# A gated cross-attention block on one core: the first half's normalised tokens turned in 32-by-32 blocks by VectorE, a query copy placed between two exponentials, two more warming products

## The chip, the core and the metric

The kernel runs on one core of one Trainium2 chip. The core has five engines that run side by side and wait for each other only through semaphores: TensorE (PE, with its weight loads shown as PEld), VectorE (DVE), ScalarE (ACT), GpSimd (POOL) and SyncE (SP), which here does nothing but issue DMAs. The metric is the device time of one execution in microseconds (us), as the median of several executions. Before the change it is 1525.99 us (three runs, 1525.85 to 1526.12).

## What is computed

There are 32 sequences of 64 tokens with 512 features, so 2,048 tokens. The block is a gated cross-attention with 32 heads of 128, followed by a gated linear layer with low-rank adapters. Cut to what matters here:

```python
x = x + tanh(g_xattn[0]) * xattn(layernorm(x), ctx, mask, bias, Wq, Wk, Wv, Wo)
x = x + tanh(g_ffn[0]) * ffn(layernorm(x), weight, bias, lora_A, lora_B, starts)

# xattn: q = x @ Wq, k = ctx @ Wk, v = ctx @ Wv  (32 heads of 128)
#        probs = softmax(q k^T / sqrt(128) + position_bias, masked); ctx = probs v; return ctx @ Wo
# ffn:   y = x @ weight^T + bias, plus (x @ A^T) @ B^T for the sequences that have an adapter
```

The second layernorm reads the result of the attention, token by token. The linear layer needs those tokens with the features on the partitions, while the attention leaves them with tokens on the partitions, so they have to be turned.

## The kernel before

The tokens are worked in two halves, p = 0 and p = 1, of 1,024 tokens (eight tiles of 128 tokens, two chunks of 512). Each half goes through three stages:

- the key stage, 16 units n = 0 to 15, one for each pair of heads (`stage_a`, first loop);
- the value stage, 16 units (`stage_a`, second loop);
- the attention, 16 pairs of heads: a query unit, the scores, a softmax, the product with the values and the product with Wo, summed into eight tiles `acc` (`attention` and its `run`).

The linear layer follows at the end of half two for all four chunks c = 0 to 3 (`ffn_chunk`): chunks 0 and 1 are the first half's tokens, chunks 2 and 3 the second half's.

Products in full precision are made of three products of split operands: `split` makes a rounded high part on ACT (`nc.scalar.copy`) and the remainder on DVE or POOL, and `mm3` (L99) multiplies high by high, high by low and low by high. A `unit` (L356, L361, L378) is one matrix product by seven block products in the order p1, p6, p7, p5, p2, p4, p3, each of six matmuls of 512 columns. The last two of a unit are carried into the next one, so that the order on PE is p1 of unit n, then p4 and p3 of unit n-1, then p6, p7, p5, p2 of unit n. DVE or ACT takes each partial sum out of PSUM. Product p4 adds into the bank (`pv`) that DVE reads after p7, and p3 into the one (`pz`) that DVE reads after p5, so PE may not start them before those reads have ended.

The order of everything beside the products is written by hand. A side job is a generator; those under way stand in the list `streams`, and `beat()`, called after each block product, runs each of them up to its next `yield`. So a job's instructions are put in between the additions of the units, one step for each block product, and `drain(job)` issues what is left of it at once. Every engine, SP too, executes its instructions in the order of issue.

What the change touches:

- **The start.** PE multiplies the identity with itself eight times (L519, `warm`) before the first real products `ppk` (L407).
- **The end of half one.** The finished tiles `acc` go to the DRAM tensor `x1d`, 128 tokens of 2 KB each. In half two's key stage `acc_stats` takes their mean and variance (from n = 3, one tile every second beat), and in its value stage `acc_rstd` makes the reciprocal roots, a chain of small operations on 128x4 tiles, one to a beat (from g = 1, L735).
- **The linear layer.** `x1_load` brings `x1d` back with tokens on partitions. For each tile `ffn_norm` normalises it on DVE (L132) into `xn`, and `ffn_tile` turns it by four TensorE transposes into PSUM (L137, `tpf`), from which ACT takes the high part (L1237) and DVE the low one (L1238). Chunk 0's tiles are turned beside the last Wo products (`beside`), those of chunk c+1 inside `ffn_chunk(c)`.
- **The first softmax of each half.** Only here are scores (L838), exponentials (L848), row sums, the division, a block-wise transpose on DVE (L876) and the copies of the turned blocks (L873, ten on ACT and six as small DVE transposes) all waited for by the very next value product `po` (L985). Beside them runs query unit 1. In that unit ACT copies the first partial sum (L361) behind both exponentials.

Of the kernel before, what the change touches and what calls it, by code (L numbers as in the profile page):

```python
# [9 lines left out]
F32 = mybir.dt.float32  # L10
# [7 lines left out]
P = 128  # L18
# [25 lines left out]
def flamingo_block(ctx: ExitStack, tc: tile.TileContext, x, xT, ctxT, bias, mask, gx, gf,  # L44
# [30 lines left out]
    ident = const.tile([P, P], F32, name="ident")  # L75
    make_identity(nc, ident)
    x1d = dram.tile([NT * P, D], F32, name="x1d")
    kd = [[dram.tile([P, 2, TP], F32, name=f"kd{p}_{n}") for n in range(NPR)] for p in range(NPH)]
    lnd = [dram.tile([2, NT, P], F32, name=f"lnd{p}") for p in range(NPH)]
    vd = [[dram.tile([P, NT, 512], F32, name=f"vd{p}_{g}") for g in range(2 * NG)] for p in range(NPH)]  # L80
# [434 lines left out]
    for _ in load_ctx(0, f, KT):  # L515
        pass
    warm = psum("warm")
    for i in range(8):
        nc.tensor.matmul(warm[:, :P], ident, ident, start=True, stop=True)  # L519
    fetch("k", 1, "r1")  # L520
    first = {}, {}
# [157 lines left out]
    def acc_rstd(p):  # L679
        for c in range(p * NCH, (p + 1) * NCH):  # L680
            yield from ln_rstd(mv2[:, c * 4:(c + 1) * 4, :], f"f{c}", rstd, c, 5)
            yield

    def stage_a(p, first, fc, res, rot, more, enter, blocks):
        xc, plain = first
        f = None
        for n in range(NPR):
            g = p * NPR + n
            if n == 0 and plain:
                sums = sum_blocks(fc, res, f"c{p}", nc.vector, xc)  # L690
                streams.append(sums)
            if n == 0 and not plain:
                drain(blocks)
            if n == (1 if plain else 0):
                streams.append(key_blocks(p, n + 1))
            if n == 3:
                f = [big(f"f{j}", [P, KT, 512], F32, f"xf{p}_{j}") for j in range(2)]
                t7 = big(rot[7], [P, 2, 1024], F32, f"wvr{p}_0a")
                t8 = big(rot[8], [P, 2, 1024], F32, f"wvr{p}_0b")
                fetch_v(p, 0, [t7[:, 0], t7[:, 1], t8[:, 0], t8[:, 1]])  # L700
                if more:
                    streams.append(paced(more, 2))
                xstat = x_stats(p)
                streams.append(xstat)
            if n == 5:
                vsum = [None] + [rwp.tile([P, 1024], F32, tag=f"r{2 + i}", name=f"vs{p}_0_{i}") for i in range(2)] + [None]
                v0 = paced(blocks_v(p, 0, rot, vsum, nc.vector, K_ORDER), 3)
                streams.append(v0)
            if 6 <= n < 6 + KT:
                for j in range(NCH):  # L710
                    nc.sync.dma_start(out=f[j][:, n - 6, :], in_=xT[p * NCH + j, n - 6])
            if n == 10:
                drain(xstat)
                x_spread(p)
            kt = k_tile(g)
            w = wt[("k", g)]

            def store(kt=kt, n=n):
                for i in range(2):
                    nc.sync.dma_start(out=kd[p][n][:, i, :], in_=kt[:, i, :])  # L720
            if n < 2 and plain:
                for j in range(2):
                    plain_half(w, plain, k_dst(kt), f"k{g}", j, plain["ps"] if n == 0 and j == 0 else None)
                store()
            else:
                if n == 2 and plain:
                    drain(sums)
                carry[:] = [unit(w, xc, None, k_dst(kt), f"k{g}", tuple(carry)), store]
        drain(v0)
        xnorm = paced(x_norm(p, f), 2)  # L730
        streams.append(xnorm)
        xq = {}
        for g in range(NG):
            if g == 1 and p:
                streams.append(acc_rstd(p - 1))  # L735
            if g == 2:
                drain(xnorm)
                streams.append(mask_stream(p))
                if p == 0:
                    streams.append(adapt)  # L740
            if g == NG - 1:
                t4 = pieces(rwp.tile([P, 1024], F32, tag="r1", name=f"x{p}t4"))
                fetch("q", p * NPR, "r0")
                bias = enter()
                streams.append(turned_blocks(f, [rot[(7 * NG + i) % 9] for i in range(7)], f"x{p}", nc.gpsimd, keep,
                                             t4, xq, bias, enter))
            for t in range(4):
                if t == 1:
                    if g + 1 < NG:
                        raw = [rwp.tile([P, 1024], F32, tag=f"r{i}", name=f"wvr{p}_{g + 1}_{i}") for i in range(4)]  # L750
                        fetch_v(p, g + 1, raw)
                        streams.append(blocks_v(p, g + 1, rot, None, nc.gpsimd, V_ORDER))
                    if g == NG - 2:
                        keep = {}
                        streams.append(turned_sums(f, f"x{p}", nc.gpsimd, keep))
                if t == 2 and g == NG - 1:
                    streams.append(prep("q", p * NPR, nc.gpsimd))
                vt = kqp.tile([P, 4, 512], F32, tag="kq", name=f"vt{p}_{g}_{t}")
                dst = {(i, j): vt[:, i * 2 + j, :] for i in range(2) for j in range(2)}
                after = unit(wt["v", p, g], xc, slice(t * P, (t + 1) * P), dst, f"v{p}_{g}_{t}", tuple(carry))  # L760

                def store(vt=vt, g=g, t=t):
                    for i in range(2):
                        for j in range(2):
                            nc.sync.dma_start(out=vd[p][2 * g + i][:, j * 4 + t, :], in_=vt[:, i * 2 + j, :])
                carry[:] = [after, store]
        enter()
        return xq


    def attention(p, res, rest, qt, freed):
# [61 lines left out]
        def scores(n, i, qT, kT):  # L833
            ps = psum(f"ps{p}_{n}_{i}", (P, NT, S))
            for t in range(NT):
                for h in range(2):
                    tok = slice(t * P + h * S, t * P + (h + 1) * S)
                    nc.tensor.matmul(ps[h * S:(h + 1) * S, t, :], qT[:, i, tok], kT[:, i, tok], start=True, stop=True)  # L838
            s = sm[n % 2][:, i]
            nc.vector.scalar_tensor_tensor(s, ps, SCALE, s, ALU.mult, ALU.add)  # L840
            mx = st.tile([P, NT], F32, tag="mx", name=f"mx{p}_{n}_{i}", bufs=4)
            nc.vector.tensor_reduce(mx, s, AX.X, ALU.max)  # L842
            nc.gpsimd.tensor_tensor(s, s, mx.unsqueeze(2).to_broadcast([P, NT, S]), ALU.subtract)  # L843
            beat()
            if n:
                streams.append(exped(s))
            else:
                nc.scalar.activation(s, s, AF.Exp)  # L848
# [48 lines left out]
        def first_softmax():  # L897
            n = 0
            tp = [rows.tile([P, NT, S], F32, tag="row", name=f"tp{p}_{n}_{i}") for i in range(2)]
            norm = normed(n, 0, (1, 0))  # L900
            next(norm)
            yield
            next(norm)
            yield
            turn(tp[1], n, 1)
            turn(tp[0], n, 0)
            yield
            for q in quads:
                copy(nc.scalar.copy, n, 1, tp[1], *q)
            for q in quads[6:]:  # L910
                copy(nc.scalar.copy, n, 0, tp[0], *q)
            for q in quads[:6]:
                copy(nc.vector.transpose, n, 0, sm[0][:, 0], *q)
            yield
            load_bias(2)
            b["m", 2] = bias_mask(2, 16)
            streams.append(b["m", 2])
# [288 lines left out]
    def ffn_weights(tags):  # L1206
        wf = [big(tags[i], [P, KT, 512], F32R, f"wf{i}") for i in range(2)]
        ffn_w.update(wf=wf, tags=tags)
        ffn_w["xn"] = big(tags[6], [P, 4, D], F32, "xn")
        ar, br, a2 = ffn_w["ar"], ffn_w["br"], ffn_w["a2"]  # L1210

        b2 = ffn_w["b2"] = [wbp.tile([P, 512], F32R, tag="wb", name=f"b2{i}") for i in range(2)]
# [18 lines left out]
    def ffn_tile(c, t):  # L1231
        if t == 0:
            act[c] = [big(ffn_w["tags"][2 + 2 * (c % 2) + i], [P, KT, 512], F32R, f"fa{c}_{i}") for i in range(2)]
        hi, lo = act[c]
        ps = transposes(ffn_w["xn"][:, t, :], f"f{c}_{t}")
        h = hi[:, :, t * P:(t + 1) * P]
        nc.scalar.copy(h, ps)  # L1237
        nc.vector.tensor_tensor(lo[:, :, t * P:(t + 1) * P], ps, h.bitcast(F32), ALU.subtract)  # L1238

    def ffn_lora(c):  # L1240
        hi, lo = act[c]
# [34 lines left out]
    def ffn_chunk(c, beside=lambda t: None):  # L1276
        more = c + 1 < NPH * NCH
        ffn_lora(c)
        for t in range(4):
            if more:  # L1280
                ffn_tile(c + 1, t)
                if t < 2:
                    ffn_norm(c + 1, t + 2)
            ffn_out(c, t)
            beside(t)
# [4 lines left out]
    for p in range(NPH):  # L1290
# [34 lines left out]
        else:  # L1325
# [16 lines left out]

            def beside(t):
                if t < 4:
                    ffn_norm(0, t)
                else:
                    moments(t - 4)
                if 1 < t < 6:
                    ffn_tile(0, t - 2)
                elif t >= 6:  # L1350
                    ffn_norm(1, t - 6)

            def rest_of(t):
                if t == 0:
# [59 lines left out]
```

## Time and profile before

| | |
|---|---|
| median of three runs | 1525.99 us |
| the profiled execution | 1527.09 us, of which the span from first to last instruction 1525.3 us |
| granted TensorE clock, mean | 1.000 |
| busy: PE / PEld / DVE / ACT / POOL | 1518.9 / 1280.3 / 940.6 / 717.1 / 1050.7 us |
| key stage of half two, 16 units | about 733 to 884 us |
| value stage of half two | about 884 to 1034 us |
| first softmax of half one / two | 323.9 to 336.8 us / 1046.9 to 1059.8 us |
| linear layer, chunks 0 to 3 | 1457.6 to 1521.6 us |

Every time is in us from the start of the span. In a timeline a row gives the start, the duration, the engine, the line, the operation, the tiles written and read, the shape and the number of instructions merged into the row; a bracket at its end gives the idle time before it and what ended that. Matmul ends are modelled and overlap, so the pace of PE is read from start to start. A full-precision matmul is recorded as two.

### The profile page before, as it was taken

How to read it: one execution, taken by the hardware profiler on the slowest of the kernel's cores; microseconds unless marked ns; L12 is line 12 of the kernel's file. 1: busy time of each engine (PE TensorE's matmuls, PEld its weight loads, DVE VectorE, ACT ScalarE, POOL GpSimd, SP SyncE). 2: the span in 40 equal slices, each digit the busy share in tenths (PEclk: the TensorE clock that was granted, in tenths of full speed). 3: DMA queues.
4: the chain of work that ended last, by engine and by line, in shares of the span. 5: the costliest groups of instructions: out<-in, count | busy, mean ns of one | idle time of the engine just before them, and what ended most of it. 6: DMA issues, size and time to landing. Idle time of an engine off the chain costs nothing.

```text
span 1525.3 us, 25057 instructions
## 1 busy us (share of the span) xinstructions
PE 1518.9 (100%) x8984; PEld 1280.3 (84%) x8984; DVE 940.6 (62%) x1579; ACT 717.1 (47%) x1582; POOL 1050.7 (69%) x1160
## 2 busy tenths in 40 slices
PE   9999999999999999999999999999999999999999
PEld 7888888888888888888888888888888888888887
DVE  5665554376677566666376557438667656666664
ACT  5444233355654664576344423335565466546511
POOL 4899378978675757668789947897867565757310
PEclk9999999999999999999999999999999999999999
DMA  5754544375335263432475454438533526353211
GB/s 207 275 195 152 190 176 168 138 286 179 123 135 184 84 230 129 165 127 87 167 271 194 152 199 167 167 139 295 185 108 139 180 87 231 126 177 116 75 42 69
DMA packets 111071, 248.51 MB, mean 163 GB/s; under 512 B 10241, under 2 KB 44033, under 8 KB 106850
## 3 DMA queue, kind: packets, MB, share of 16 engines
q1 hardware_dynamic: 110658, 246.38, 45.9%
q8 instruction: 71, 1.16, 0.3%
q10 hardware_dynamic: 288, 0.52, 0.1%
q14 instruction: 54, 0.44, 0.1%
HBM read 173.45 MB, written 73.42 MB: 162 GB/s over the span
## 4 chain that ended last, share of the span: by engine, by line
PE 98%; DVE 1%; ACT 1%; POOL 0%; issue 0%; DVEq 0%; POOLq 0%
PE pa L99 23%; PE po L985 8%; PE pzv L99 6%; PE pvv L99 6%; PE pxv L99 6%; PE pxq L99 5%; PE pvq L99 5%; PE pzk L99 5%; PE pvk L99 5%; PE pxk L99 5%; PE pzq L99 5%; PE ps L838 4%; PE pf L99 3%; PE pyv L99 3%; PE pyq L99 3%; PE pyk L99 3%
## 5 line engine op out<-in xcount | busy, mean ns | idle before, releaser
L99 PE MATMUL pa<-wo,ch 128*128 128x512 f32 x896 | 278.4, 392 | 0.0
L873 ACT COPY pt<-tp 32x256 f32<-32x256 f32 x452 | 182.4, 404 | 62.2 <-DVE tp L876 51.7
L99 PEld LDWEIGHTS pa<-wo,ch 128*128 128x128 f32 x896 | 166.5, 188 | 34.6
L99 PE MATMUL pa<-wo,cl 128*128 128x512 f32 x448 | 174.6, 390 | 0.0
L1034 DVE TENSOR_TENSOR acc<-pa,acc 128x512 f32<-128x512 f32 x192 | 129.9, 682 | 56.1 <-PE pa L99 56.1
L791 POOL TENSOR_TENSOR sm<-sm,madd 128x512 f32<-128x512 f32 x60 | 77.2, 1296 | 88.5 <-DMA sm<-bias 88.5
L865 POOL TENSOR_TENSOR sm<-sm,r 128x512 f32<-128x512 f32 x64 | 67.0, 1046 | 76.5 <-DVE r L864 75.8
L985 PEld LDWEIGHTS po<-pt,v 128*128 128x128 f32 x960 | 111.5, 192 | 3.7 <-ACT pt L873 1.6
L985 PE MATMUL po<-pt,v 128*128 128x128 f32 x960 | 112.7, 275 | 0.8 <-ACT pt L873 0.8
L843 POOL TENSOR_TENSOR sm<-sm,mx 128x512 f32<-128x512 f32 x64 | 67.1, 1049 | 62.1 <-DVE mx L842 61.9
L356 DVE TENSOR_TENSOR vt<-pvv,vt 128x512 f32<-128x512 f32 x64 | 44.1, 689 | 93.4 <-PE pvv L99 93.3
L990 DVE TENSOR_TENSOR cl<-po,ch 128x512 fp32r<-128x512 f32 x112 | 76.7, 691 | 39.5 <-ACT ch L989 39.1
L99 PEld LDWEIGHTS pa<-wo,cl 128*128 128x128 f32 x448 | 84.1, 188 | 17.8
L356 DVE TENSOR_TENSOR qT<-pvq,qT 128x512 f32<-128x512 f32 x64 | 44.2, 690 | 73.6 <-PE pvq L99 73.5
L989 ACT CAST ch<-po 128x512 fp32r<-128x512 f32 x112 | 65.9, 590 | 50.1 <-PE po L985 48.1
L356 DVE TENSOR_TENSOR kT<-pvk,kT 128x512 f32<-128x512 f32 x60 | 41.3, 688 | 75.2 <-PE pvk L99 75.1
L90 POOL TENSOR_TENSOR wo<-rawo,wo 128x512 fp32r<-128x512 f32 x56 | 71.2, 1296 | 15.0 <-ACT wo L89 15.0
L378 ACT COPY vt<-pxv 128x512 f32<-128x512 f32 x32 | 18.8, 589 | 131.0 <-PE pxv L99 131.0
L852 ACT ACTIVATE sm<-sm 128x512 f32<-128x512 f32 x60 | 38.0, 633 | 79.1 <-POOL sm L843 79.1
L356 DVE TENSOR_TENSOR qT<-pzq,qT 128x512 f32<-128x512 f32 x64 | 44.2, 690 | 37.9 <-PE pzq L99 37.6
L192 POOL TENSOR_TENSOR vs<-wvr,wvr 128x512 f32<-128x512 f32 x24 | 31.7, 1332 | 48.2 <-DMA wvr<-wv 48.1
L838 PEld LDWEIGHTS ps<-kB,qT 128*64 128x64 f32 x2048 | 61.2, 138 | 3.6 <-issue 1.4
(1001 smaller groups left out, 3916.6 us busy)
## 6 DMA issues: line engine op xcount, KB each, us to landing
kd<-kT SPq DMA_DIRECT2D x64, 512.0 KB, 4.0
vd<-vt SPq DMA_DIRECT2D x128, 256.0 KB, 2.4
kB<-kd SPq DMA_DIRECT2D x32, 1024.0 KB, 9.9
v<-vd SPq DMA_DIRECT2D x32, 1024.0 KB, 7.7
rawq<-wq SPq DMA_DIRECT2D x32, 512.0 KB, 3.3
sm<-bias SPq DMA_DIRECT2D x64, 256.0 KB, 3.8
rawo<-wo SPq DMA_DIRECT2D x32, 512.0 KB, 3.5
rawk<-wk SPq DMA_DIRECT2D x31, 512.0 KB, 5.3
```

Source lines behind the costliest of these rows:

```text
L90: eng.tensor_tensor(lo, raw, hi.bitcast(F32), ALU.subtract)
L99: nc.tensor.matmul(ps, a, b, start=start and i == 0, stop=stop and i == len(todo) - 1, skip_group_check=True)
L356: nc.vector.tensor_tensor(o, ps, i, ALU.add)
L791: nc.gpsimd.tensor_tensor(t, t, masks[p][0], ALU.add)
L838: nc.tensor.matmul(ps[h * S:(h + 1) * S, t, :], qT[:, i, tok], kT[:, i, tok], start=True, stop=True)
L843: nc.gpsimd.tensor_tensor(s, s, mx.unsqueeze(2).to_broadcast([P, NT, S]), ALU.subtract)
L865: nc.gpsimd.tensor_tensor(t, t, r.unsqueeze(2).to_broadcast([P, NT, S]), ALU.mult)
L873: f(pts[n == NPR - 2][dst, i, :, src], of[src, :, ki * 32:(ki + 1) * 32])
L985: nc.tensor.matmul(ps[:, t * P:(t + 1) * P], b["v", n][:, c * 4 + t, i * P:(i + 1) * P], pts[n == NPR - 2][:, i, c * 4 + t, :], start=True ...
L989: nc.scalar.copy(h[:, i, sl], ps)
L990: nc.vector.tensor_tensor(lo[:, i, sl], ps, h[:, i, sl].bitcast(F32), ALU.subtract)
L1034: nc.vector.tensor_tensor(acc[t], ps, acc[t], ALU.add)
```

## The change

Three things are changed.

First, the tokens of the first half are normalised and turned in half two's key stage. From n = 6 `acc_rstd` runs there (no longer in the value stage). From n = 10 `acc_turned` takes the eight tiles in turn: a load from `x1d`, three beats later the normalisation and one DVE transpose of the 128x512 tile, which turns each 32x32 block in itself, and then a store into a new DRAM tensor `xtd`. Before the linear layer `ffn_load` reads `xtd` for one chunk with 16 DMAs whose access pattern puts the blocks into place, in runs of 32 numbers (128 bytes), and `ffn_given` splits what came into high and low part. Chunks 0 and 1 so need neither `ffn_norm` nor `ffn_tile`. Chunks 2 and 3 are as before.

Second, in the first softmax of each half the second exponential becomes a stream. It is issued at the next beat, behind the query unit's first copy. The transpose of head 1's tile is issued one beat earlier than that of head 0.

Third, ten warming products stand where there were eight.

```diff
+    xtd = dram.tile([NT, P, D], F32, name="xtd")
...
-    for i in range(8):
+    for i in range(10):
         nc.tensor.matmul(warm[:, :P], ident, ident, start=True, stop=True)
...
+    def acc_turned(p):
+        def store(t, tp):
+            nc.sync.dma_start(out=xtd[t], in_=tp)
+
+        tp = None
+        for t in range(NT):
+            c = p * NCH + t // 4
+            xt = rows.tile([P, D], F32, tag="row", name=f"xr{p}_{t}")
+            nc.sync.dma_start(out=xt, in_=x1d[t * P:(t + 1) * P, :])
+            yield
+            if tp is not None:
+                store(t - 1, tp)
+            yield
+            yield
+            ln_apply(xt, xt, mv2[:, c * 4:(c + 1) * 4, :], rstd[c], t % 4)
+            tp = rows.tile([P, D], F32, tag="row", name=f"xq{p}_{t}")
+            nc.vector.transpose(tp, xt)
+            yield
+            yield
+        store(t, tp)
...
+            if n == 6 and p:
+                drain(more)
+                streams.append(acc_rstd(p - 1))
             if n == 10:
                 drain(xstat)
                 x_spread(p)
+            if n == 10 and p:
+                turned_acc = acc_turned(p - 1)
+                streams.append(turned_acc)
...
         drain(v0)
+        if p:
+            drain(turned_acc)
...
-            if g == 1 and p:
-                streams.append(acc_rstd(p - 1))
...
             beat()
-            if n:
+            if n or not i:
                 streams.append(exped(s))
             else:
                 nc.scalar.activation(s, s, AF.Exp)
...
             next(norm)
-            yield
             turn(tp[1], n, 1)
+            yield
             turn(tp[0], n, 0)
             yield
...
-        ffn_w["xn"] = big(tags[6], [P, 4, D], F32, "xn")
+        streams.append(ffn_load(0))
...
+    def ffn_load(c):
+        ffn_w["xt"] = big(ffn_w["tags"][6], [P, KT, 512], F32, f"xt{c}")
+        blocks = xtd[c * 4:(c + 1) * 4].rearrange("t (i b) (k a j) -> k a b (t i) j", b=32, a=4, j=32)
+        for kt in range(KT):
+            for a in range(4):
+                nc.sync.dma_start(out=ffn_w["xt"][a * 32:(a + 1) * 32, kt, :].rearrange("b (t j) -> b t j", j=32),
+                                  in_=blocks[kt, a])
+            yield
+
+    def ffn_given(c, kt):
+        if kt == 0:
+            act[c] = [big(ffn_w["tags"][2 + 2 * (c % 2) + i], [P, KT, 512], F32R, f"fa{c}_{i}") for i in range(2)]
+        split(ffn_w["xt"][:, kt, :], act[c][0][:, kt, :], act[c][1][:, kt, :], nc.vector)
...
-            if more:
+            if c + 1 < NCH:
+                for kt in range(KT)[2 * t:2 * t + 2]:
+                    ffn_given(c + 1, kt)
+                if t == 1:
+                    ffn_w["xn"] = big(ffn_w["tags"][6], [P, 4, D], F32, "xn")
+            elif more:
                 ffn_tile(c + 1, t)
...
                 if t < 4:
-                    ffn_norm(0, t)
+                    ffn_given(0, t)
                 else:
                     moments(t - 4)
-                if 1 < t < 6:
-                    ffn_tile(0, t - 2)
-                elif t >= 6:
-                    ffn_norm(1, t - 6)
+                if t == 3:
+                    streams.append(ffn_load(1))
```

## The prediction

> **What bounds the kernel now.** I read the page's busy times and its chain of waits first, then timelines of the four places that the change touches.
>
> ```profile
> span 1525.3 us, 25057 instructions
> ...
> PE 1518.9 (100%) x8984; PEld 1280.3 (84%) x8984; DVE 940.6 (62%) x1579; ACT 717.1 (47%) x1582; POOL 1050.7 (69%) x1160
> ...
> PE 98%; DVE 1%; ACT 1%; POOL 0%; issue 0%; DVEq 0%; POOLq 0%
> ```
>
> PE is the path. A product taken off PE, or a wait of PE, is worth its full length; work elsewhere is free until PE waits for it. Now PE in the linear layer, chunk 0 (with transposes) and chunk 3 (without):
>
> ```profile
> 1459.38 0.60 PE L137 MATMUL tpf<-ident,xn 128*128 128x128 f32 x4
> 1459.73 3.02 PE L99 MATMUL pf<-wf,fa 128*128 128x512 f32 x12
> ...
> 1463.04 0.60 PE L137 MATMUL tpf<-ident,xn 128*128 128x128 f32 x4
> ...
> 1508.69 2.88 PE L99 MATMUL pf<-wf,fa 128*128 128x512 f32 x12
> ...
> 1511.86 2.88 PE L99 MATMUL pf<-wf,fa 128*128 128x512 f32 x12
> ```
>
> A tile lasts 3.66 us with its four transposes and 3.17 without. ACT in half two's first softmax:
>
> ```profile
> 1050.77 0.63 ACT L848 ACTIVATE sm<-sm 128x512 f32<-128x512 f32 x1 [4.87 <-POOL sm L843]
> 1052.31 0.63 ACT L848 ACTIVATE sm<-sm 128x512 f32<-128x512 f32 x1 [0.91 <-POOL sm L843]
> 1052.85 0.57 ACT L361 COPY qT<-pxq 128x512 f32<-128x512 f32 x1
> ```
>
> The copy, whose product was done by 1050.6, stands behind an exponential that waits for POOL. DVE's addition behind it (L356) starts at 1053.45, and the block copies at 1056.43. PE's weight loads show the end of that chain:
>
> ```profile
> 1055.83 1.22 PEld L99 LDWEIGHTS pvq<-x1p,wq17p 128*128 128x128 f32 x6 [0.26 <-DVE qT L356]
> 1057.74 1.23 PEld L99 LDWEIGHTS pzq<-x1p,wq17p 128*128 128x128 f32 x6 [0.69 <-DVE qT L356]
> 1059.79 0.30 PEld L985 LDWEIGHTS po<-pt,v 128*128 128x128 f32 x2 [0.83 <-ACT pt L873]
> ```
>
> These three are nearly all the waits that PE has. Last, five units of half two's key stage, n = 6 to 10 (columns: PE, PEld, DVE, ACT, POOL busy):
>
> ```profile
> 785.80:795.30 9.50, 9.50 (x44) 7.86 (x43) 6.79 (x14) 4.14 (x10) 8.83 (x13) 1.00 0.76 263
> 795.30:804.80 9.50, 9.50 (x44) 7.86 (x43) 7.71 (x16) 3.93 (x10) 9.34 (x13) 1.00 0.58 205
> 804.80:814.30 9.50, 9.50 (x44) 7.86 (x43) 7.97 (x15) 4.56 (x11) 9.34 (x12) 1.00 0.68 237
> 814.30:823.80 9.50, 9.50 (x44) 7.86 (x43) 4.95 (x7) 4.95 (x12) 8.89 (x13) 1.00 0.64 221
> 823.80:833.40 9.60, 9.60 (x44) 7.96 (x43) 6.93 (x13) 4.58 (x12) 8.72 (x12) 1.00 0.47 164
> ```
>
> DVE has 1.5 to 4.5 us free in a unit of 9.52, and POOL next to nothing.
>
> **What the Trainium skill says.** "TensorE: Matmul & The Clock Gate", Part 1: the array starts at half clock and is released after about 3.4 us of sustained work, by a window that runs on its own. The trace agrees on two speeds: a weight load lasts 333 ns in the first warming products and 188 later; here the change lies between loads at 6.62 (0.34 us) and 7.41 (0.19), over 5 us after the first product. "SBUF — State Buffer", section "Who interferes with whom": DVE operations in a two-port mode (such as `tensor_scalar`) or with two SBUF inputs exclude GpSimd, and the loser blocks fully. The trace fits: the same small DVE operation (L126) takes 153 to 1203 ns, the same POOL operation (L299) 0.74 or 1.26 us. "VectorE: DVE Perf Modes", "The three transpose paths": DVE turns 32x32 blocks only; here 128x512 takes 0.70 us (L876). "DMA: Bandwidth & Descriptors", Specifications: line rate needs runs of 512 bytes; priced below.
>
> **A, transposes off PE.** Removed are eight groups of four. Four stood beside the Wo products: 1433.77 to 1457.56 is 23.79 us for eight tiles, where a tile without transposes takes 2.72 (1418.54 to 1421.26), so 2.03 us. Four stood in chunk 0: 4 x (3.66 - 3.17) = 1.96. Sum 3.99; I take 3.9. The eight normalisations (0.54 us) leave this stretch too. The eight ACT and DVE splits stay, now from SBUF (DVE 0.69 from PSUM; 0.65 to 0.7 for L90 from SBUF), beside products as before.
>
> Their data: SP issues chunk 0's 16 DMAs behind the value load of 1409.31, so from about 1410, and the next Wo fetch is held by POOL until 1425.94 anyway. At 0.65 us of SP each (the adapter load L1198, 512 runs of 192 bytes) that is 10.4 us, over by 1421; the first use is at 1438. Chunk 1's may start once DVE has read chunk 0's, about 1446 with the groups before it gone, and are issued by 1457. Chunk 1's first products stand at 1474.0, then 1470. The price of a packet: from 1390 to 1398 the DMA engines were busy 0.73 x 8 us x 16 = 93 us, from 1409 to 1417 0.61 x 8 x 16 = 78 us. Both hold 1.5 MB of the same loads; the first also has the adapter loads. Of the 15 us difference the 96 packets of 2 KB take about 9 (11,200 us of engine time for 248.5 MB is 22 GB/s), so the 512 small ones 6, some 12 ns each. A chunk is 8192 packets, 512 to an engine: 6 us, less than their issue. I take no cost; the upper bound is the page's mean packet, 101 ns (11,200 us / 110,658), under rivals.
>
> **B, first softmax.** ACT copies at 1051.42 behind the first exponential, done at 1051.99; the second stays at 1052.31, POOL's date. DVE: addition py at 52.60 instead of 53.45; row sum of head 0 (needs the second exponential, 1052.94) at 53.30, its factor ready at 54.41 instead of 55.17; transpose of head 1 (POOL's division ended 1053.74) at 54.43 to 55.14; addition pv to 55.85 (before 55.78); transpose of head 0 after POOL at 55.59, 55.88 to 56.59; addition pz to 57.27 (before 57.68). ACT's eight block copies of head 1 take 3.32 us: 55.17 to 58.49 instead of 59.75. PE then: p4 at 55.9, p3 at 57.4, end 58.8. So `po` starts at 58.8 instead of 59.79. Head 0's six DVE copies (2.65) end at 59.95, its two on ACT at 59.3, before PE needs them at 60.6. What is late next is PE itself. Gain 1.0 per half, twice: 2.0. Bounds: 0.4 a half (only pz's date) to 1.3 (all waits gone: 1046.96 + 2.0 + 7 x 1.36 = 1058.5).
>
> **C, two more warming products.** Eight take 3.78 us, 0.45 each from start to start. At a clock that changes at a date of its own, two at half clock displace 0.9 us of real products at that clock, worth 0.45 at full. The first real one starts at 4.71, right behind the eighth, so no wait covers it; PE has none after it until the first softmax. Cost 0.45. Bounds: -0.4 (the first data come late in other executions, or the clock earlier), +0.9.
>
> **D, the new DVE work in the key stage.** `acc_rstd`: 30 small operations, about seven a unit, n = 6 to 9. In the value stage 31 of its kind take 13.9 us, 0.45 each; alone 0.15, behind a POOL operation about 0.67. At 0.45, 3.2 us a unit: 10.0, 10.9, 11.1, 8.1 against 9.52. DVE falls behind by 0.5, 1.9, 3.5, then gains. PE starts p4 three products (4.08 us) after p7, and the addition takes 0.69, so it tolerates 3.3 us. Cost 0.2 at that price, nothing at 0.15; at 0.67 (4.7 a unit) the excess is 8.1, the cost 4.8. Part of DVE's idle time cannot be used, so I take 1.0. `acc_turned`: 8 x (0.54 + 0.70) = 9.9 us over six units, 1.7 each, on units of 5 to 7: fits. On SP it adds eight loads and eight stores of 256 KB. The normalisation is three beats (4.1 us) behind its load; today's loads from x1d (L1182, into x1t) land in 5.5 us, at worst 8.2. So DVE can stand still for 2 to 4 us with the additions behind it; from n = 10 it has that much free. Behind the store on SP wait the kd stores and the next raw key weights, whose fetch at 831.26 (5.3 us to land) is read by ACT at 837.55: one us of margin, and the unit that uses them begins at 844. Taken at nothing beyond the 1.0, at most 2 more. The value stage loses `acc_rstd`, where PE waited for nothing: no gain.
>
> **Sum.** -3.9 - 2.0 + 0.45 + 1.0 = -4.45. The profiled execution, 1527.09 (span 1525.3 and 1.8 around it), becomes 1522.6; the median, 1.1 lower, 1521.5. About 0.2% (3.05 us) is what a measurement of this kernel can tell from no change.
>
> **Rivals.**
> - DVE becomes the bound in units 7 to 10 (small operations near 0.67, or loads that land late): D costs 3 to 4.8, the sum is about -2: 1524. For it: POOL at 9.34 of 9.5 just there. Against: two small operations in a row often share one wait (0.15 for the second). Chance 0.18.
> - The softmax gains only 0.4 a half, as DVE's order gives back what the copy wins: 1522.7. Against: every date above is read from a row. Chance 0.08.
> - Slower: the 128-byte packets, 512 to an engine and chunk, each at the page's mean of 101 ns. Chunk 0 would land at 1410 + 52 + 2 = 1464, chunk 1, which may only start then, near 1519; its products would begin at 1520 instead of 1470: about 1571. It costs from 40 ns a packet ((1470 - 1446 - 3.3) / 512) and takes the whole gain from 49. Against: the 12 ns above; for: those runs were adjacent in DRAM, these lie 2 KB apart. Chance 0.06.
> - PE loses over 7 us in the key stage to late loads: 1529. Chance 0.03.
>
> **How the numbers follow.** The forecast has 0.65 (own range 1519.5 to 1522.9: down with B at 1.3 a half and C and D at nothing, up with D at 2.4). Faster: 0.65, 0.06 of the second rival and 0.01 of the first, 0.72. Same: 0.17 of the first and 0.02, 0.19. Slower: 0.09. Range 1519.5 to 1525.0: it takes in the first rival.
>
> **What would show it.** Right: 32 records of `tpf` instead of 64, tiles of 2.72 and 3.17 us at the end; `po` 11.8 us after the scores instead of 12.83; `ppk` 0.9 us later; PE waiting for DVE by about 1 us at 805 to 830. Wrong: `pt` or `fa` waiting for the DMA of `xt`, or long waits of `pvk` and `pzk` for `kT`.

## The result, and the profile after

The changed kernel takes 1520.47 us in the median (1519.78 to 1520.89, six runs) where the kernel before took 1526.05 beside it (1525.85 to 1526.88): ratio 0.9962, 95% interval 0.9949 to 0.9974. Its profiled execution took 1520.39. Forecast was 1521.5.

The page of the changed kernel, the lines that answer to the first fence of the prediction, with the row of the main DMA queue (packets, MB, share of 16 engines):

```profile
span 1518.6 us, 25096 instructions
...
PE 1513.4 (100%) x8956; PEld 1278.3 (84%) x8956; DVE 941.6 (62%) x1587; ACT 717.7 (47%) x1582; POOL 1051.1 (69%) x1160
...
q1 hardware_dynamic: 129858, 252.67, 48.1%
...
PE 100%; POOL 0%; DVE 0%; DVEq 0%; issue 0%; POOLq 0%
```

PE has 28 instructions fewer in the records (32 transposes go, four half products of warming come), 5.5 us less of busy time, and the chain of waits is now PE alone: the span fell by 6.7 us, so about 1.2 us of the gain was waiting, as far as modelled ends can tell. The view of waits, kept to PE, has a single row left; before it also named `po` for ACT and `pzq` for DVE:

```profile
PE warm L520 <- POOL ident masks.py:199: 1.3, 1, 1.3
```

The fullest two of the four units of half two's key stage in which VectorE got its small operations (columns as in the prediction: PE, PEld, DVE, ACT, POOL busy):

```profile
795.30:804.80 9.50, 9.50 (x44) 7.87 (x43) 8.87 (x21) 3.49 (x10) 8.51 (x11) 1.00 0.56 196
804.80:814.30 9.50, 9.50 (x44) 7.87 (x43) 9.46 (x24) 4.55 (x12) 8.74 (x13) 1.00 0.71 248
```

Over all four (785.80 to 823.80) DVE has 34.44 us of work instead of 27.42, and in the second of these two it is as good as full. PE still shows 9.50 in each, and by the starts of its products it lost nothing there. From the first key product of half two to its first scores product it takes 314.16 us in both kernels (732.80 to 1046.96 before, 731.22 to 1045.38 after).

The chain of waits in the softmax of half one and in the second chunk of the linear layer (start, us, what):

```profile
323.71 2.02 PE ps L868 x64
...
334.12 1.36 PE pzq L100 x6
335.48 3.57 PE po L1015 x32
...
1467.39 0.23 PE pt L1290
...
1469.21 0.44 PE tpf L138 x4
...
1483.83 0.23 PE pt L1290
```

Products follow one another from the scores to `po`, at 1.36 us for six, where before the chain went over DVE, POOL and ACT. The interval from `pt` to `pt` is 16.44 us where four groups of `tpf` remain, as here; in the first chunk, now without them, it is 14.51 (1452.89 to 1467.39).

The difference of the two profiled executions, place by place: start 0.25 us (the row of 78 `ppk` products begins at 10.87 instead of 11.12), softmax 1.33 a half, 2.66 (from the first scores product to the first of the Wo products that follow: 17.35 us instead of 18.68), key stage 0, transposes 3.87 (measured alone below). Sum 6.8, of 6.7 in the spans.

### The profile page after: what moved, and what is told of

Same layout as the page of the kernel before. It is cut to its first block, busy times and chain, and to the rows that moved or that the text cites. A ratio compares the mean times of both kernels' runs of the same rounds, so it can differ in the third digit from the quotient of the medians.

```text
span 1518.6 us, 25096 instructions
## 1 busy us (share of the span) xinstructions
PE 1513.4 (100%) x8956; PEld 1278.3 (84%) x8956; DVE 941.6 (62%) x1587; ACT 717.7 (47%) x1582; POOL 1051.1 (69%) x1160
## 2 busy tenths in 40 slices
DMA packets 130271, 254.79 MB, mean 168 GB/s; under 512 B 27393, under 2 KB 61185, under 8 KB 126050
## 3 DMA queue, kind: packets, MB, share of 16 engines
q1 hardware_dynamic: 129858, 252.67, 48.1%
## 4 chain that ended last, share of the span: by engine, by line
PE 100%; POOL 0%; DVE 0%; DVEq 0%; issue 0%; POOLq 0%
PE pa L100 23%; PE po L1015 8%; PE pxq L100 6%; PE pvq L100 6%; PE pzv L100 6%; PE pvv L100 6%; PE pxv L100 6%; PE pzq L100 6%; PE pzk L100 5%; PE pvk L100 5%; PE pxk L100 5%; PE ps L868 4%; PE pf L100 3%; PE pyq L100 3%; PE pyv L100 3%; PE pyk L100 3%
## 5 line engine op out<-in xcount | busy, mean ns | idle before, releaser
L357 DVE TENSOR_TENSOR vt<-pzv,vt 128x512 f32<-128x512 f32 x64 | 44.2, 691 | 33.1 <-PE pzv L100 32.4
## 6 DMA issues: line engine op xcount, KB each, us to landing
kB<-kd SPq DMA_DIRECT2D x32, 1024.0 KB, 10.3
```

The source lines that it names most:

```text
L357: nc.vector.tensor_tensor(o, ps, i, ALU.add)
```

## Experiments

Ratios are to the kernel before on the same chip; what is smaller than a run's noise is read from stretches of the trace.

**The two edits of the softmax, each alone in the kernel before.** First the copy between the exponentials:

```diff
-            if n:
+            if n or not i:
                 streams.append(exped(s))
```

> The kernel before with one edit of the change alone: the second exponential of a half's first softmax goes to the streams, so that ScalarE's copy of the next query tile runs ahead of it. Read: time from the first scores product to the first po product in both halves (before 12.83 us, changed kernel 11.7), and the time. Theory 1 (the copy's 1.22 us and the wait behind it is what the softmax loses; the turn order alone brings nothing): 11.7 in both halves, 2.2 us faster in all, ratio about 0.9985. Theory 2 (each edit brings its half, as the two waits lie one behind the other): 12.2, 1.1 us faster. Theory 3 (only the turn order counts): 12.8, no difference.

Measured: 1524.27 us (1523.83 to 1525.23), ratio 0.9987 (0.9981 to 0.9994). Then the order of the turns:

```diff
-            yield
             turn(tp[1], n, 1)
+            yield
             turn(tp[0], n, 0)
```

> The kernel before with the other edit alone: the first turn of the second pair is issued one step earlier, ahead of the step's end instead of after it. Read as in the run with the copy alone. Theory 1 (the copy is all of it): 12.8 us from scores to po, no difference in time. Theory 2 (half each): 12.2 and 1.1 us faster. Theory 3 (the turn order is all of it): 11.7 and 2.2 us faster, ratio about 0.9985.

Measured: 1525.16 us (1524.68 to 1525.91), ratio 0.9991 (0.9983 to 1.0). The chain of waits of the kernel with the copy alone, half one, where `po` is released:

```profile
335.36 0.41 ACT pt L873
...
335.82 3.84 PE po L985 x32
```

And with the turn order alone, where `pvq` is:

```profile
331.75 0.59 DVE qT L356
...
332.38 1.66 PE pvq L99 x6
```

A chain dates a row from the modelled end of what came before it, or, after a wait, from its own first start. So the dates of `po` in two chains can't be compared to a tenth or two, and the starts on PE's timeline are taken. Half one, the kernel before and then the changed kernel, with the addition of which `pzq` waits:

```profile
334.74 1.65 PE L99 MATMUL pzq<-x0p,wq1p 128*128 128x512 f32 x6 [0.26 <-DVE qT L356]
336.79 3.84 PE L985 MATMUL po<-pt,v 128*128 128x128 f32 x32 [0.39 <-ACT pt L873]
340.55 2.08 PE L838 MATMUL ps<-kB,qT 128*64 128x64 f32 x64
...
332.81 0.65 DVE L357 TENSOR_TENSOR qT<-pzq,qT 128x512 f32<-128x512 f32 x1
...
333.95 1.52 PE L100 MATMUL pzq<-x0p,wq1p 128*128 128x512 f32 x6
335.31 3.73 PE L1015 MATMUL po<-pt,v 128*128 128x128 f32 x32
338.98 2.08 PE L868 MATMUL ps<-kB,qT 128*64 128x64 f32 x64
```

From start to start, in us (the first scores products start at 323.89, 323.89, 322.84 and 323.64):

| kernel | scores to `po` | `po` to the next scores | scores to the Wo products |
|---|---|---|---|
| before | 12.90 | 3.76 | 18.68 |
| copy alone | 11.93 | 3.76 | 17.71 |
| turn order alone | 12.43 | 3.66 | 18.10 |
| both | 11.67 | 3.67 | 17.35 |

With the copy alone a block copy of ACT still releases `po`. With the turn order alone the addition for `pvq` comes behind a turn, and PE waits for that. With both PE waits for nothing. The 0.1 us of the third column lies at the first product of `po`: where `po` was waited for, its second product starts 0.21 us after the first, and otherwise 0.11 to 0.13, nearly the distance of all the others (0.11). The gain is 0.97, 0.58 and 1.33 a half; the second half gives the same within 0.02. None of the three theories held as written: each edit has a share of its own, 0.2 us of which they have in common, and the copy's is the larger.

**The turning alone.** The kernel before with parts A and D and neither the softmax nor the warming edits.

> The kernel before with the turning of the first half's tokens by VectorE alone (the key stage's new work, the loads back, the casts), without the softmax and warming edits. Theory: 32 of the 64 transposes of TensorE go, eight groups at 0.49 us, and the key stage of half two stays at 314.2 us: 3.9 us faster, ratio 0.9974. Rival 1 (VectorE's small operations hold TensorE back in units 7 to 10 once the softmax doesn't hide them): 2.9 us or less. Rival 2 (the small packets of the loads cost TensorE time beside the Wo products): gain under 2 us, with the interval from pt of chunk 0 to pt of chunk 1 over 14.5 us.

Measured: 1522.30 us (1522.06 to 1523.09), ratio 0.9973 (0.9963 to 0.9983): 4.06 us faster. The Wo stretch takes 21.77 us to the first `pt`, 23.71 before; the first chunk 14.51 instead of 16.44: 1.94 + 1.93 = 3.87. The key stage took 314.16. Both rivals fall. The softmax in this kernel kept its 18.68 us, so that its waits didn't pay for the key stage.

**More small operations in the key stage.** An unused second chain of the same kind, beside the first:

```diff
+    def acc_again(p):
+        for c in range(p * NCH, (p + 1) * NCH):
+            yield from ln_rstd(mv2[:, c * 4:(c + 1) * 4, :], f"g{c}", {}, c, 4)
+            yield
...
                 streams.append(acc_rstd(p - 1))
+                streams.append(acc_again(p - 1))
```

> The changed kernel with the chain of small VectorE operations in half two's key stage issued twice, from the same step on (the second chain's results are not used). It adds 32 small operations in units 7 to 10, where the changed kernel's VectorE had 7.0 us more to do than before. Theory as it stands after the first look (a small operation is worth 0.25 us there, the lag that the stage bears is some 3.3 us): about 7 us more VectorE work over four units with 17 us of room, lag stays under 3.3 us, TensorE loses 0 to 0.5 us, key stage of half two 314.2 to 314.7. Prediction's price (0.45 us each): 14 us more, 1 to 3 us lost. Rival (VectorE is the bound in these units): all of it on top, 5 us or more.

Measured: 1520.14 us (1519.63 to 1521.08), ratio 0.996 (0.9946 to 0.9973). The same two units:

```profile
795.30:804.80 9.50, 9.50 (x43) 7.87 (x42) 9.50 (x25) 3.50 (x10) 9.34 (x13) 1.00 0.39 152
804.80:814.30 9.50, 9.50 (x43) 7.63 (x42) 9.50 (x34) 4.46 (x12) 6.53 (x9) 1.00 0.82 276
```

DVE is without a break in both, and to the scores it is 314.35 us, 0.19 more than in the changed kernel. The whole of it lies in the second of these units, where p3's weights waited for an addition that stood among the small operations:

```profile
806.35 0.68 DVE L357 TENSOR_TENSOR kT<-pzk,kT 128x512 f32<-128x512 f32 x1
...
807.14 1.22 PEld L100 LDWEIGHTS pzk<-c1p,wk23p 128*128 128x128 f32 x6 [0.33 <-issue]
```

Over the four units DVE has 29 instructions more than in the changed kernel (106 to 77), and only 1.9 us more busy time (36.30 to 34.44), less than the 7 expected. The 26 operations of the second chain among them do last 7.3 us, 0.28 each, but they overlap with their neighbours, and the first chain's got shorter, so busy time gives no price. That twice the chain costs 0.2 us does, and that is within the theory.

**Less time for the turned tiles' loads.** One step between a tile's load and VectorE's first use of it:

```diff
             nc.sync.dma_start(out=xt, in_=x1d[t * P:(t + 1) * P, :])
             yield
-            if tp is not None:
-                store(t - 1, tp)
-            yield
-            yield
             ln_apply(xt, xt, mv2[:, c * 4:(c + 1) * 4, :], rstd[c], t % 4)
...
             yield
             yield
+            store(t, tp)
+            yield
+            yield
-        store(t, tp)
```

> The changed kernel with one step instead of three between the load of a tile to be turned and VectorE's first use of it (a step is some 2 us there; the store of the turned tile comes two steps after its turning, so three steps before the buffer's next use, one more than in the changed kernel). In the changed kernel the load took 3.7 us to land and VectorE stood 4.9 us for the loads and 1.8 us for the stores over the eight tiles, with no loss on TensorE; in the run with 4 warming products it stood 11.9 us and TensorE lost 0.94 us in the key stage. Theory (the loss comes when VectorE's waits for its own loads and stores pile up): VectorE waits 2 to 3 us for each load, 16 to 24 us in all, and TensorE loses 1 to 4 us, key stage of half two 315 to 318 instead of 314.16. Rival (VectorE's lag is borne by the eight PSUM buffers however the waits lie, and the 0.94 us had another cause, the late raw weights of GpSimd): 314.2 to 314.5 with the same waits.

Measured: 1529.79 us (1528.57 to 1531.06), ratio 1.0022 (1.0013 to 1.003), slower than the kernel before. PE's rows in the view of waits:

```profile
PE pzk L100 <- DVE kT L357: 3.7, 1, 3.7
PE pvk L100 <- DVE kT L357: 2.7, 1, 2.7
```

And DVE on the timeline (start, us; in brackets its idle time ahead and what ended it):

```profile
845.98 0.68 DVE L357 TENSOR_TENSOR kT<-pvk,kT 128x512 f32<-128x512 f32 x1
850.07 0.55 DVE L133 TENSOR_SCALAR xr<-xr,mv,yf 128x512 f32<-128x512 f32 x1 [3.41 <-DMA xr<-x1d]
...
851.28 0.65 DVE L357 TENSOR_TENSOR kT<-pzk,kT 128x512 f32<-128x512 f32 x1
```

DVE stands 3.41 us for a load with the addition for `pzk` queued behind it, and five us pass between two additions of which PE needs one every 2 us or so. Over the eight tiles DVE stood 17.0 us for loads; to the scores it took 322.66 us, 8.5 more. The direction is the theory's, the size over twice its 1 to 4. PE's two waits are 6.4 of it. They had a second price that the theory left out: behind them TensorE ran at half speed again, with a granted clock of 0.57 (the column behind POOL's):

```profile
852.00:856.00 4.00, 3.92 (x10) 3.12 (x11) 2.51 (x5) 1.79 (x5) 3.51 (x5) 0.57 0.44 131
```

That is an estimate of 1.7 us (0.43 of 4.0).

**Fewer and more warming products.**

> The changed kernel with the 8 warming products of before instead of 10. Read in the chain of waits: the start of the row of 78 ppk products (before 11.12 us, after 10.87). Model from these two: up to a date T the PE runs at half speed, a warming product is 0.23 us at full speed, so the row starts at 5.56 + 0.23 x products + T/2; before gives T = 7.4, after T = 6.0. Theory (T has nothing to do with the number of products and scatters between executions by up to 1.4 us): start between 10.4 and 11.1, whatever T comes up, and by the times 0.46 us faster than the changed kernel with equal T, so a ratio of 0.9997 and no difference that can be told. Rival (each two products more bring T forward by 1.4 us): T = 7.4 again, start 11.1, and 0.25 us slower than the changed kernel.

Measured: 1520.24 us (1519.91 to 1520.68), ratio 0.9959 (0.9945 to 0.9973); the row begins at 10.71 us, so T = 6.6. Both are as the theory has it; the rival's 11.1 and 7.4 are not.

> The changed kernel with 16 warming products. Theory (T is independent of the number, 6.0 to 7.4): the row of 78 ppk products starts at 12.2 to 12.9 us, 1.4 us later than in the changed kernel for six products at 0.23 us, if T is equal. Rival (more products bring T forward): T at or under 6.0, start at 12.2 or earlier, so only a start clearly under 12.2 speaks for it here.

Measured: 1521.81 us (1520.89 to 1522.41), ratio 0.9969 (0.9959 to 0.998); the row begins at 12.37, T = 6.3. From 8 to 16 products the row comes 1.66 us later and the median 1.57: some 0.2 us for a product. The start is again the theory's.

> The changed kernel with 4 warming products. Theory (T is independent of the number, 6.0 to 7.4): the row of 78 ppk products starts at 9.5 to 10.2 us unless another wait takes over (operands of ppk not there yet: then the chain shows a wait of PE for DVE in the first 10 us and the start stays near 10.9). Rival (each two products bring T forward by 1.4 us): T about 10, start about 11.5, 0.6 us later than in the changed kernel.

Measured: 1521.53 us (1520.79 to 1522.39), ratio 0.9968 (0.9957 to 0.998). The start of its chain of waits:

```profile
0.71 3.88 DMA c<-ctxT
...
4.64 3.78 PE ppk L408 x4
8.42 1.78 PE ppk L100 x6
...
11.92 17.71 PE ppk L100 x78
```

The first operand comes at 4.6 us; four products are over at 3.4, PE stands for 1.2 us, and the first two rows of real work run slowly. The weight loads date full speed:

```profile
8.65 0.33 PEld L100 LDWEIGHTS ppk<-c0p,wk0a 128*128 128x128 f32 x1
9.08 0.22 PEld L100 LDWEIGHTS ppk<-c0p,wk0a 128*128 128x128 f32 x1
9.34 0.19 PEld L100 LDWEIGHTS ppk<-c0p,wk0a 128*128 128x128 f32 x1
```

It comes within the load of 9.08, at about 9.2, some 4.5 us after the gap. Taken alone, this start of 11.92 us is nearer to the rival's 11.5 than to the theory's 10.2, or 10.9 with a wait; the runs with 8 and 16 products speak against the rival, and only this one has a gap. The reading that fits all three is that work without a break dates full speed, and that the gap starts the count anew; it rests on this one execution. The start explains 1.05 us of this execution's 2.0 over the changed kernel's; the other 0.94 lies in the key stage, which took 315.10. DVE stood 11.9 us there for loads and stores of turned tiles (`xr` 9.1, `xq` 2.8) against 6.7 in the changed kernel (4.9 and 1.8). PE lost 0.54 of it in unit n = 13, behind an addition of DVE that came late, and 0.40 in n = 14, for want of key weights that POOL splits and of which the raw form had landed late:

```profile
860.27 0.41 ACT L296 CAST wk30p<-rawk 128x256 fp32r<-128x256 f32 x1 [1.60 <-DMA rawk<-wk]
...
868.00 0.77 PEld L100 LDWEIGHTS pyk<-c1p,wk30p 128*128 128x128 f32 x4 [0.53 <-POOL wk30p L300]
```

The fetch stands on SP behind the stores of keys, and it landed 2.7 us later in the stage than in the changed kernel. So the rival in the expectation for one step between load and use is right for 0.40 of the 0.94. The edit is far from that stage, so the loss is taken for chance, which no run shows: of the nine profiled executions with the changed kernel's turning and its pace, it is the only one where the turned tiles are seen to have cost PE anything in the key stage. In the others DVE stood 6.7 to 9.8 us for them, and all but the run with the doubled chain, whose loss came before the first tile was loaded, took 314.15 to 314.16 us to the scores.

**The second chunk's loads later in the program.**

> The changed kernel with the 16 small-packet loads of the second chunk issued in one go at the end of the Wo products instead of one by one from tile 3 on. In the changed kernel their issue took 8.4 us from 1443.4, the landing 2.3 us, and the casts of the chunk began at 1456.6 while pt of chunk 1 came at 1467.2. Theory (12 ns a packet): issue from about 1452, 8 to 10 us, landed by 1464, four casts and subtractions of 0.6 and 0.7 us behind the landing, ready about 1465: TensorE waits 0 to 1 us, the interval from pt of chunk 0 to pt of chunk 1 14.5 to 15.5. Rival (packets of 128 bytes cost 40 ns or more when nothing else is in their way): landing some 9 us later than that, the interval 20 us or more.

Measured: 1519.72 us in one execution. The view of the tile's DMA issues:

```profile
L1276 SPq DMA_DIRECT2D xt<-xtd x32: 319/487/2771, 1406.4 to 1450.6; - x32
```

In the changed kernel the row reads 1407.0 to 1451.3; take off the 0.65 us by which this execution started earlier, and the issues are where they were. The loads stand later in the program but no later in time: on SP nothing else was in their way, and the free buffer dated them (DVE's last reading of the first chunk's tile ends at 1443.4 us in the changed kernel and at 1442.7 here, and the first of the second chunk's loads is issued in the same tenth). The run tells nothing of the packets, and the test of that deadline stays undone.

**The last chunk turned too.** A step further in the same way: tiles 4 to 7 of half two normalised and turned by VectorE two at a time beside the second chunk, read back by 16 loads.

```diff
+    def ffn_turn(t):
+        xr, tp = [rows.tile([P, D], F32, tag="row", name=f"x{nm}3_{t}") for nm in "rq"]
+        ln_apply(xr, x1_row(3, t), mv2[:, 12:16, :], rstd[3], t)
+        nc.vector.transpose(tp, xr)
+        nc.sync.dma_start(out=xte[t], in_=tp)
...
+            def turn_of(t):
+                if t < 2:
+                    ffn_turn(2 * t)
+                    ffn_turn(2 * t + 1)
+                else:
+                    ffn_load3([t - 2])
```

> The changed kernel with the last chunk of tokens (tiles 4 to 7 of half two) turned in the same way: normalised and turned by VectorE during the second chunk's products, stored, and read back by 16 small-packet loads into a free buffer during the second and third chunk, so 16 more transposes leave TensorE. Theory: four groups of 0.49 us, the third chunk's interval from pt to pt 14.51 us instead of 16.44, 1.95 us faster than the changed kernel, ratio to the kernel before 0.9950. Rival 1 (VectorE then has 4 more normalisations and turnings, 6 us, in the second chunk, and the stores of the output wait behind 16 load issues of some 0.65 us on SP): a wait of TensorE for VectorE or for an output buffer appears and takes 1 us or more of it. Rival 2 (the turned tiles come back too late): TensorE waits for the casts ahead of the fourth chunk.

Measured: 1520.03 us (1519.4 to 1520.63), ratio 0.9959 (0.9945 to 0.9972). The view of PE's waits has a new row:

```profile
PE pt L1307 <- DVE fa L1269: 1.3, 1, 1.3
```

The chain of waits shows what stands behind it:

```profile
1479.95 0.72 DVE xq L1289
1480.69 1.99 DMA xte<-xq
1483.41 0.55 DVE fa L1269
```

The third chunk did fall to 14.57 us. But with two row buffers the second turn of each pair waits for the first one's store, 3.1 us in all, and the subtraction that the third chunk needs stands behind it. So the first rival's wait came, by a store and not by the amount of work.

**The same with slower steps.** The last version with 8 warming products, and with the stream that turns the first half's tokens at half its pace:

```diff
-                turned_acc = acc_turned(p - 1)
+                turned_acc = paced(acc_turned(p - 1), 2)
```

> The changed kernel with the last chunk turned too, with 8 warming products, and with two steps for each one of the stream that turns the first half's tokens, so that each load has some 12 us to land and each store 8. Theory: VectorE's waits for xr and xq loads and stores fall to under 1 us in all, the key stage is 314.16 us, warming costs 0.46 us less than with 10 products at equal clock date, so 2.4 us faster than the changed kernel, 1518.0, ratio to the kernel before 0.9947. Rival (something later in the key stage collides with the longer stream, a row buffer or the stores of keys): key stage over 314.3 and no better than the version with the last chunk alone.

Measured: 1530.22 us (1528.89 to 1530.77), ratio 1.0024 (1.0015 to 1.0033). Its row of PE's waits:

```profile
PE pvv L101 <- DVE vt L358: 7.8, 1, 7.8
```

At half pace the eight tiles don't fit: the stage ends with the stream unfinished, the rest is issued in one go (`drain`), DVE stands 11.0 us for loads that it has only just asked for, and the first additions of the value stage wait behind it. To the scores it took 324.49 us. The mistake is the opposite of the version with one step and costs still more, 10.3 us against 8.5. Here too the wait cost the clock: from 899.1 to 903.9 the granted one was 0.51, an estimate of 2.4 us. The rival was nearer than the theory.

**One tile at a time.** The last chunk's turning spread over the second chunk, its 16 loads all beside the third, the old pace in the key stage, 8 warming products:

```diff
                 if t < 2:
                     ffn_norm(c + 1, t + 2)
+                if c == 1:
+                    ffn_turn(t)
```

> The changed kernel with the last chunk of tokens turned by VectorE too, now one tile beside each tile of the second chunk instead of two at a time, and with 8 warming products. In the version that turned two at a time VectorE stood 3.1 us for the store of the first of each pair (there are two row buffers), and TensorE waited 1.3 us for its casts ahead of the third chunk; the third chunk itself came from 16.44 to 14.57 us. Theory: with 3.6 us between the turnings, the stores (2 us to land) are out of the way, so TensorE doesn't wait at pt of the third chunk, 1.9 us less than the changed kernel; with the two warming products fewer 0.46 us more: about 2.3 us faster than the changed kernel, ratio to the kernel before 0.9948. Rival (the 16 loads, whose issue takes 10 us on SP, come too late once they start only with the third chunk): TensorE waits 1 to 2 us ahead of the fourth chunk, and the time stays at that of the changed kernel.

Measured: 1517.66 us (1517.53 to 1517.88), ratio 0.9941 (0.9928 to 0.9955), against 0.9962 for the change. PE's only wait is again that of the start; the third chunk takes 14.51 us (1483.29 to 1497.80), as the theory has it, and the rival's wait ahead of the fourth didn't come. The median is 2.8 us under the changed kernel's and the profiled execution 2.5 (0.54 at the start and 1.93 in the third chunk), where 2.3 was expected. It is the fastest of the versions here.

## Why the prediction was near, by its steps

**A** was right in mechanism and size: 3.9 taken, 3.87 in the trace of the turning alone, 4.06 by its time. The small packets cost no time. They can be priced from the rows of the main queue: 45.9% of 1525.3 us before, 48.1% of 1518.6 after, so some 485 us more over 16 engines. The changed kernel has 19,200 packets more, of which the page puts 17,152 under 512 bytes (27,393 to 10,241). The other 2,048 at the page's mean of 101 ns take 207, and 278 remain: an estimate of 16 ns for a small one, where the prediction estimated 12. The third rival needed 40.

**B** had the right mechanism and was under: 2.0 taken, 2.66 measured, which is its own upper bound of 1.3 a half, all waits gone. The forecast still let PE wait a little for DVE: the addition `pz` was to end at 1057.27 and p3 to start behind it at 1057.4. In the changed kernel that addition ends 9.82 us after the first scores product (332.81 + 0.65), at 1056.7 by the forecast's clock, and p3 follows p4 without a wait, at 1057.2. So `po` starts 1.23 us a half earlier, not 1.0. DVE was dated late because its instructions were laid end to end. On the timeline before, the addition `py` runs from 330.45 to 331.14 and the row sum behind it starts at 331.06; some 0.1 us of this kind at each of five steps makes the half microsecond. The other 0.10 a half is the first product of `po`, which no longer follows a wait. The `po` date of 11.8 us came out (11.77) only because it was read in the chain, where the date before was a start and the one after a modelled end.

**C** had the right price and the wrong sign for this pair of executions. A product costs about 0.2 us by the runs with 8 and 16, so two cost 0.4, near the forecast's 0.45. But the date T of full speed was 7.4 us in the profiled execution before and 6.0 in that after, and half of the 1.4 us outweighs them. By the model that the expectation states, T is 7.4, 7.5, 5.4, 7.2, 6.6, 6.1 and 5.9 in the seven profiled executions with 8 products, 6.0, 5.7, 6.0, 6.2 and 4.7 in the five with 10, and 6.3 with 16: no order by number that could be told from scatter, though the mean is 6.6 with 8 and 5.7 with 10. The Trainium skill, "TensorE: Matmul & The Clock Gate", Part 1, says that the window is some 3.4 us of time, not a number of products, and that it runs freely, so that its phase differs from run to run. One full window after the first product at 1.34 us would end 3.4 to 6.8 us on, an estimate from the page's figure; T lies 3.4 to 6.1 us on, which agrees. The page also has the change vary by half a microsecond to either side from run to run; here it varied by 2.7, and the measurement decides.

**D** is the term that failed: 1.0 taken, nothing measured. The price of a small operation was nearly right: the 26 of the 30 that lie in these four units last 0.40 us in the mean, against 0.45. (DVE's busy time rises by only 7.0 us, as they overlap with their neighbours and the small operations that were there before take 5.1 us instead of 7.2.) At 0.45 the prediction's own working gave 0.2, as it reckoned that PE bears a lag of DVE of 3.3 us. What failed is the 0.8 added to it because part of DVE's idle time could not be used: DVE used it up to 9.46 of 9.50 us, without a loss, and twice the chain cost 0.19. So the first rival's small operations were no bound.

The half of D that had been put at nothing, the turned tiles, is where the danger lies: DVE stood for its loads and stores in every such execution, 6.7 us in the changed kernel, and one with 11.9 lost 0.94. Of that, 0.40 came by the fetch of key weights, the path to which the prediction had given one us of margin. Shown is that this cover is thin (one step instead of three loses 8.5), not how often the changed kernel itself loses by it.

With the measured terms the sum is -3.87 - 2.66 + 0.45 + 0 = -6.1, where the medians differ by 5.6 and the profiled spans by 6.7. For the spans T accounts for the rest (C is -0.25 there and not 0.45); for the other executions T isn't on record, and its scatter is only large enough to do so. B and D together were too dear by 1.7 us; that the median came out only 1.0 from the forecast is luck.

## What to carry to other kernels

In this kernel an engine that was nearly full took more work without a loss, as long as it came in operations of at most 1.1 us each; a wait for a transfer is what harmed, as everything behind it on that engine waits too, and if TensorE then stands for long enough, its clock falls as well. So count the steps between a load and its use, and see that the stream ends within its stage. When several instructions of an engine are dated ahead, go by their distance from start to start: durations laid end to end made the additions half a microsecond late here. A date that scatters between executions, as that of the clock here, has to be read from several before a difference in it is put down to an edit.

## What the runs showed of the hardware that was not expected

- Full speed of TensorE came between 4.7 and 7.5 us after the start of thirteen executions whose first products followed without a break, which alone moves a kernel's time by up to 1.4 us; in the one execution with a gap of 1.2 us it came at 9.2. By these runs the use of warming is to bridge the time until the first operand is there (4.6 us): eight products reach to 5.1, four end at 3.4.
- A DMA with runs of 128 bytes took 0.49 us of SP in the median to issue (0.32 to 2.26) and landed 2.3 us later (2.0 to 7.7); 16 of them per chunk, 8192 packets, went by beside TensorE without a trace in its time.
- DVE doing without a break what it is given for two units of 9.5 us cost PE 0.19 us; standing for loads, up to 5.4 us at a time and 17.0 in all, cost it 8.5.
- After waits of 2.7 and 3.7 us, 1.6 us apart, TensorE ran at half speed for some 3.4 us, and after one of 7.8 us for 4.8; after waits of under 0.7 us in the key stage (four warming products) its weight loads kept their 0.19 us.
